# A recommender kernel: categories picked by matmuls, more history tiles fetched row by row, and a loop body of 90 l instead of 45

## The chip, the cores and the metric

One core of a Trainium2 chip runs the kernel. The metric is the device time of one execution in microseconds (us); lower is better. Before the change the median of ten runs was 51,484.07 us (51,445.77 to 51,514.49).

## The reference, cut to what matters

For 16,384 users the kernel computes a small recommender network. `hist` holds 200 (called L, index l) past items for every user.

```python
u, it, c = u_emb[user], i_emb[item], c_emb[cate]          # rows of 64 f32
h = i_emb[hist]                                           # (200, 16384, 64)
feat = concat([h, it, h - it, h * it])
a = dice(feat @ au_W1 + au_b1, au_alpha, axis=1)          # normed over all users
w = a @ au_W2 + au_b2
cur = sum(w * h, axis=0)                                  # over the 200 items
z = concat([u, it, c, cur])
z = dice(z @ W1 + b1, ...); z = dice(z @ W2 + b2, ...)
return z @ W3 + b3
# dice(x): p = sigmoid((x - mean) * rsqrt(var + 1e-8)); x * (p + alpha * (1 - p))
```

The tables of users and items have 100,000 rows of 256 bytes, the table of categories 1,000.

## The kernel before, in words

The users are cut into 128 tiles of 128. A step `k` handles one of 8 columns (`ND`, index c) of 16 tiles (`TD`) for one l: `l, c = divmod(k, ND)`. There are 200 x 8 = 1,600 steps.

**Two ways to fetch rows.** `fetch` (L123 by way of `gather`) asks GpSimd (POOL) for a whole tile with one indirect DMA: 128 rows by a list of indices. `rows_by_address` (L293 and L301) fetches tiles row by row: it loads 16 to 20 addresses into registers (L293, one instruction), and then issues one DMA of 256 bytes per row (L301: a MOVE and the DMA). Half of a step's rows go to SyncE's queue (SP), half to ScalarE's own (ACT). The last tile of the columns in `SIDES = (1, 3, 4, 5, 6, 7)` is fetched in this way, column 5 (`SOMETIMES`) only where l is a multiple of 3 (`EACH`); otherwise its last tile is gathered with indices loaded by `load_side_ids` (L142). So an l has six tiles by address (96 rows a step, 48 per queue) or five (80 rows, 40 per queue). The rows land in three buffers `side` used in turn. `place` waits on ACT until the 128 rows have landed (L311) and copies the tile into the column's buffer (L352). A row for a buffer waits until the tile that lay there has been copied out. There are five column buffers `rows`; POOL fetches for step k + 4 as soon as the transposes have emptied one.

**One step** (`step`), in the order written out by hand (`manual_schedule`), each engine in order:
- POOL gathers the 15 or 16 tiles of step k.
- ACT: `hidden(k-2)` copies px out with the bias (L339), `gate(k-9)` is a sigmoid (L328), `place(k-1)`, then the rows of step k.
- SP: only the rows of step k; at the start of an l the index list of the next (L136), at its third step the addresses (L145).
- DVE (VectorE): four transposes of step k-1's column (`turn`, L156), statistics (L344), `product` (L360), y (L331), the weighted sum (L335, L336).
- PE (TensorE): for k-1 the matmuls into ph and px, for k-9 those into wb (all L161).

At the end of an l `moments` joins the statistics. `scale_and_shift` then has ACT take a square root (L170), for which ACT loads another table of functions and afterwards the old one again, and DVE a reciprocal (L171).

**Stages.** The start gathers all 128 item tiles and turns them. The loop has bodies of `LPB = 45` l, so it runs four times to l = 180; the last 20 l stand after it, and with their last steps the head begins. The head gathers 128 tiles of categories and 128 of users, one column of each in turn, and runs the three layers.

Of the kernel before, what the change touches and what calls it, by code (L numbers as in the profile page):

```python
# [14 lines left out]
P = 128  # L15
# [4 lines left out]
CD = 2 * CH  # L20
LPB = 45
ROWS = 5
# [4 lines left out]
SOMETIMES = 5  # L27
EACH = 3
LOAD = 20
ROW = 4 * D  # L30
U8 = mybir.dt.uint8
# [3 lines left out]
def din_kernel(  # L35
# [75 lines left out]
    idx = [make(f"idx{i}", P, NC, dt=I32) for i in range(IDX)]  # L111
    ids = [make(f"ids{i}", P, NT, dt=I32) for i in range(3)]
    side = [make(f"side{i}", P, D) for i in range(3)]
# [15 lines left out]

    def load_ids(t, v):  # L130
        nc.sync.dma_start(t[:, :NC], columns(v))
        for s in range(NS):
            nc.sync.dma_start(t[:, NC + s : NC + s + 1], col(v[(NC + s) * P : (NC + s + 1) * P]))

    def load_hist_ids(i, l):
# [7 lines left out]

    def load_addresses(i, l):
        nc.sync.dma_start(addr[i], r_hist[ds(l, 1), NC * P :])  # L145

# [20 lines left out]
    def scale_and_shift(mean, var, rstd, shift):  # L167
        n = mean.shape[0]
        std = small.tile([P, 1], F32, tag="std", name="std")
        nc.scalar.activation(std[:n], var, AF.Sqrt, bias=eps[:n])  # L170
        nc.vector.reciprocal(rstd, std[:n])  # L171
        nc.vector.scalar_tensor_tensor(shift, mean, -1.0, rstd, ALU.mult, ALU.mult)

    eps = make("eps", P, 1)
    blk_h = make("blk_h", P, P)
# [13 lines left out]
    def attention_weights():  # L189
        nc.vector.memset(eps, EPS)  # L190
        for t in (blk_h, blk_i, blk_m, blk_p, au_bias, au_al, au_w2):
# [44 lines left out]
    def head_weights():  # L236
# [3 lines left out]
        for e in range(2):  # L240
            for g in range(2):
                r, d = quarter(e, g), ts(e, S)
                nc.sync.dma_start(w1a[r, :, ts(g, ZA)], w1[d, :, :ZA])
                nc.sync.dma_start(w1b[r, :, ts(g, ZB)], w1[d, :, ZA:])
        for g in range(2):
            nc.sync.dma_start(w2a[ts(g, ZA), g * ZA : g * ZA + Z2], W2[:ZA])
            nc.sync.dma_start(b1a[ts(g, ZA)], col(b1)[:ZA])
            nc.sync.dma_start(ala[ts(g, ZA)], col(alpha1)[:ZA])
            nc.sync.dma_start(b1b[ts(g, ZB)], col(b1)[ZA:])
            nc.sync.dma_start(bias2[g * ZA : g * ZA + Z2], col(b2))  # L250
            nc.sync.dma_start(al2[g * ZA : g * ZA + Z2], col(alpha2))
            for j in range(4):
                r = slice(j * S + g * ZB, j * S + (g + 1) * ZB)
                nc.sync.dma_start(w2b[r, j, g * ZA : g * ZA + Z2], W2[ZA:])
                w = j * S + g * ZO
                nc.sync.dma_start(w3[g * ZA : g * ZA + Z2, j, w : w + ZO], W3)
                nc.sync.dma_start(alb[r], col(alpha1)[ZA:])
# [8 lines left out]

    flat = i_emb.rearrange("v d -> (v d)").bitcast(U8)


# [3 lines left out]
    def tiles_by_address(l):  # L273

        round_, i = divmod(l, EACH)
        first = round_ * (EACH * (NS - 1) + 1) + i * (NS - 1) + (i > 0)
        return first, [j for j, c in enumerate(SIDES) if has_side(l * ND + c)]

    def rows_by_address(k):
        l, s = divmod(k, ND)  # L280
        first, tiles = tiles_by_address(l)
        n = len(tiles) * P // ND // 2
        loads = -(-n // LOAD)
        for i, (engine, issue) in enumerate(
            ((mybir.EngineType.SP, nc.sync), (mybir.EngineType.Activation, nc.scalar))
        ):
            r0, end = (2 * s + i) * n, (2 * s + i + 1) * n
            while r0 < end:
                many = min(end - r0, -(-n // loads))
                at0 = tiles[r0 // P] * P + r0 % P  # L290
                while tiles[(r0 + many - 1) // P] * P + (r0 + many - 1) % P != at0 + many - 1:
                    many -= 1
                _, at = nc.values_load_multi_w_load_instructions(  # L293
                    addr[l % 3][:, at0 : at0 + many],
                    engines=(engine,), min_val=0, max_val=ROW * (V - 1),
                    skip_runtime_bounds_check_because="the DMA checks the address against the table",
                )
                for r, a in enumerate(at, r0):
                    m, p = first + r // P, r % P
# [7 lines left out]
                r0 += many  # L307

    def await_rows(m):
        if m in keys:  # L310
            fence = nc.scalar.wait_ge(landed[m % 3], 16 * P)  # L311
            tc.declare_fence(fence.ins, group=keys.pop(m))
            nc.scalar.sem_clear(landed[m % 3])

    def has_side(k):
        l, c = divmod(k, ND)
        return c in SIDES and (c != SOMETIMES or l % EACH == 0)

# [27 lines left out]
    def place(k):  # L346
        if has_side(k):
            l, c = divmod(k, ND)
            first, tiles = tiles_by_address(l)
            m = first + tiles.index(SIDES.index(c))  # L350
            await_rows(m)
            nc.scalar.copy(rows[k % ROWS][:, TD - 1], side[m % 3])  # L352

# [28 lines left out]

    def step(k, last=None):

# [6 lines left out]
        if has(k - 2):  # L391
            hidden(k - 2)
            if ends:
                measure(k - 2)
                moments((k - 2) // ND)
        if has(k - LAG):
            gate(k - LAG)
        if has(k - 1):
            place(k - 1)
        if has(k):  # L400
            rows_by_address(k)
        if has(k - 1):
            turn(k - 1)
        if has(k - 2) and not ends:
            measure(k - 2)
        if has(k - 1):
            product(k - 1)
        if has(k - LAG):
            weights(k - LAG)
            weigh(k - LAG)  # L410

    def steps(l0, n, end):
        for k in range(n * ND):
            l, c = divmod(k, ND)
            if c == 0 and l + 1 < end:
                load_hist_ids((l + 1) % IDX, l0 + l + 1)
                if (l + 1) % EACH:
                    load_side_ids((l + 1) % IDX, l0 + l + 1)
            if c == 2 and l + 1 < end:
                load_addresses((l + 1) % 3, l0 + l + 1)  # L420
            if c == 4 and l + 1 < end:
                scale_addresses((l + 1) % 3)
            step(k)

    with tc.manual_schedule():
        load_ids(ids[0], r_item)
        load_hist_ids(0, 0)
        load_addresses(0, 0)
        load_ids(ids[1], r_cate)
        load_ids(ids[2], r_user)  # L430
        nc.gpsimd.iota(lanes, pattern=[[1, P]], base=P, channel_multiplier=-1)
        attention_weights()
        for t in (*hT, *xs, *side, hm):
            nc.vector.memset(t, 0.0)
        for t in curT:
            nc.vector.memset(t, 0.0)
# [4 lines left out]
        for c in range(1, 2 * ND):  # L441
            nc.vector.tensor_copy(stats[-1 % 3][:, c, :], stats[-1 % 3][:, 0, :])
        scale_addresses(0)
        layer(px, [(blk_m, hm)])

        for c in range(ND + 1):
            if c < ND:
                for n in range(TD):
                    j = column(c, n)
                    gather(rows[c % ROWS], ids[0][:, j : j + 1], n, i_emb)  # L450
            if c:
                transpose(itT[c - 1], rows[(c - 1) % ROWS])
        nc.vector.memset(rows[-1 % ROWS], 0.0)
        head_weights()
# [15 lines left out]

    def head_fetch(k, j):
        c, u = divmod(j, 2)
        for n in range(TD):
            i = column(c, n)
            gather(rows[k % ROWS], ids[1 + u][:, i : i + 1], n, (c_emb, u_emb)[u])

    def head_layer(j):
        c, u = divmod(j, 2)
        if u == 0:
            pairs = ((2, ucT[j % 4]), (1, itT[c]), (3, curT[c]))  # L480
        else:
            pairs = ((0, ucT[j % 4]),)
        layer(px, [(w1a[:, f], t) for f, t in pairs], first=not u, last=u == 1)
        layer(ph[:S], [(w1b[:, f], t) for f, t in pairs], first=not u, last=u == 1)
        if u:
            nc.scalar.activation(za[c], px, AF.Identity, bias=b1a)
            measure_head(0, c, za[c])
            nc.scalar.activation(zb[c // 4][ts(c % 4, S)], ph[:S], AF.Identity, bias=b1b)
            if c % 4 == 3:
                measure_head(1, c // 4, zb[c // 4])  # L490

    with tc.manual_schedule():
        steps(BODY, L - BODY, L - BODY)
        for j in range(2 * ND + 2):
            if j < 2 * ND:
                head_fetch(K + j, j)
            step(K + j, last=K - 1)
            if 1 <= j <= 2 * ND:
                transpose(ucT[(j - 1) % 4], rows[(K + j - 1) % ROWS])
            if j >= 2:  # L500
                head_layer(j - 2)

# [98 lines left out]
```

## Time and profile before

| what | us |
|---|---|
| the profiled execution, in all | 51,433.07 |
| its span, first to last instruction | 51,431.3 |
| median of ten runs | 51,484.07 |
| PE busy | 20,762.5 (40%) |
| DVE busy | 15,101.0 (29%) |
| ACT busy | 4,417.6 (9%) |
| POOL busy | 23,569.5 (46%) |
| first history row on SP | 113.2 |
| last history row on SP | 51,005.4 |

Issuing a DMA does not count as busy. The queue of an engine is written with a q: SPq, ACTq. A row of the table of groups names the line, the engine, the operation, out<-in and its count; after the bar busy time in us and the mean ns of one; after the next bar how long the engine had been idle before it, and what ended that idle time. A row of the waits says who waited for whom, the total in us, how often, and the longest wait. A row of a timeline has start and duration in us, and instructions that follow one another are merged; the bracket at its end is idle time before it.

### The profile page before, as it was taken

The page shows a single profiled execution, that of the slowest core. Times are in us where ns is not written, and L with a number is a line of the kernel's source. Part 1 is how long each engine was busy: PE and PEld are TensorE (multiplying, and loading weights), DVE is VectorE, ACT ScalarE, POOL GpSimd, SP SyncE. Part 2 cuts the span into 40 slices and gives each one's busy share as a digit, 9 for nine tenths or more (in the row PEclk, how much of TensorE's full clock was granted, in tenths as well). Part 3 has the DMA queues.
Part 4 walks back from the last instruction along what each step waited for, and adds up shares of the span by engine and source line. Part 5 has one row for each costly group of instructions (what it writes and reads, how often), then busy time and mean ns, then how long its engine had stood idle before and what let it go on. Part 6 is the DMA issues. An engine that isn't in the chain of part 4 may idle for free. (4 is left out here: it accounts for less than half of the span.)

```text
span 51431.3 us, 423966 instructions
## 1 busy us (share of the span) xinstructions
PE 20762.5 (40%) x38856; PEld 8517.7 (17%) x38856; DVE 15101.0 (29%) x18955; ACT 4417.6 (9%) x4941; POOL 23569.5 (46%) x24922
## 2 busy tenths in 40 slices
PE   3444444443443444334444444344344444434444
PEld 1111111111111111111111111111111111111111
DVE  2222222232222222222222222222222222222223
ACT  0000000000000000000000000000000000000001
POOL 5444444444444444444444444444444444444444
PEclk7666666666766666666666666666666666666667
DMA  0000000000000000000000000000000000000000
GB/s 19 18 17 17 18 17 17 17 17 18 17 18 17 17 18 17 17 17 18 17 17 18 17 17 18 17 17 17 17 17 18 17 17 18 17 17 18 17 17 17
DMA packets 1130924, 894.71 MB, mean 17 GB/s; under 512 B 729024, under 2 KB 729024, under 8 KB 1127896
## 3 DMA queue, kind: packets, MB, share of 16 engines
q0 software_dynamic: 797344, 818.07, 7.2%
q1 hardware_dynamic: 193112, 31.56, 0.3%
q10 hardware_dynamic: 137440, 17.76, 0.2%
q14 instruction: 2722, 22.30, 0.1%
q8 instruction: 306, 5.01, 0.0%
HBM read 865.10 MB, written 0.13 MB: 17 GB/s over the span
## 5 line engine op out<-in xcount | busy, mean ns | idle before, releaser
L123 POOL DMA_INDIRECT rows<-in_L_rec_i_emb,idx x24400 | 23080.0, 946 | 27451.5 <-DVE hT L156 19846.3
L161 PE MATMUL ph<-hT,unit 128*128 128x512 f32 x6404 | 5963.1, 1087 | 30114.0 <-DVE hT L156 29704.1
L335 DVE SCALAR_TENSOR_TENSOR wb<-wb,au_bias,hT 128x1024 f32<-128x1024 f32 x1609 | 2079.8, 1293 | 23201.1 <-remote 20171.3
L161 PEld LDWEIGHTS ph<-hT,unit 128*128 128x128 f32 x6404 | 1798.8, 311 | 33173.9 <-DVE hT L156 32512.6
L156 DVE STREAM_TRANSPOSE hT<-rows 64x512 f32<-64x512 f32 x6404 | 4516.7, 705 | 8958.0 <-ACT rows L352 8814.3
L339 ACT ACTIVATE xs<-px,au_bias 128x1024 f32<-128x1024 f32 x1602 | 1785.1, 1114 | 45384.5 <-issue 40195.8
L161 PE MATMUL px<-hT,blk_h 128*128 128x512 f32 x6404 | 4014.5, 714 | 291.5 <-issue 153.2
L161 PE MATMUL px<-itT,blk_i 128*128 128x512 f32 x6404 | 3417.9, 616 | 0.0
L161 PE MATMUL wb<-xs,blk_x 128*128 128x512 f32 x6436 | 3294.0, 593 | 47.7 <-DVE curT L336 45.5
L161 PE MATMUL wb<-y,blk_p 128*128 128x512 f32 x6436 | 3294.6, 593 | 37.3 <-DVE y L331 30.6
L161 PE MATMUL px<-hm,blk_m 128*128 128x512 f32 x6408 | 3012.9, 592 | 69.9 <-remote 69.9
L344 DVE BATCH_NORM_STATS2 st<-xs 128x6 f32<-128x512 f32 x3204 | 2061.3, 686 | 1959.4 <-ACT xs L339 1586.0
L360 DVE TENSOR_TENSOR hm<-ph,itT 128x1024 f32<-128x1024 f32 x1601 | 1958.0, 1223 | 1727.0 <-PE ph L161 1159.4
L161 PEld LDWEIGHTS px<-hT,blk_h 128*128 128x128 f32 x6404 | 1601.2, 252 | 2779.0 <-issue 2491.6
L336 DVE TENSOR_TENSOR curT<-wb,curT 128x1024 f32<-128x1024 f32 x1609 | 1970.0, 1224 | 54.8
L331 DVE TENSOR_TENSOR y<-pg,xs 128x1024 f32<-128x1024 f32 x1609 | 1953.9, 1214 | 12.6 <-issue 12.5
L328 ACT ACTIVATE pg<-xs,sh,rs 128x1024 f32<-128x1024 f32 x1609 | 1934.1, 1202 | 28.4 <-DVE y L331 13.9
L161 PEld LDWEIGHTS px<-itT,blk_i 128*128 128x128 f32 x6404 | 1388.7, 217 | 1958.0 <-issue 1958.0
L161 PEld LDWEIGHTS wb<-xs,blk_x 128*128 128x128 f32 x6436 | 1224.1, 190 | 1593.1 <-issue 1543.8
L161 PEld LDWEIGHTS wb<-y,blk_p 128*128 128x128 f32 x6436 | 1224.7, 190 | 1583.4 <-issue 1546.4
L161 PEld LDWEIGHTS px<-hm,blk_m 128*128 128x128 f32 x6408 | 1218.1, 190 | 1605.7 <-issue 1534.6
L352 ACT COPY rows<-side 128x64 f32<-128x64 f32 x1068 | 251.2, 235 | 668.3 <-DMA side<-in_L_rec_i_emb 573.9
(155 smaller groups left out, 2148.4 us busy)
## 6 DMA issues: line engine op xcount, KB each, us to landing
side<-in_L_rec_i_emb SPq DMA_DIRECT2D x68288, 0.2 KB
side<-in_L_rec_i_emb ACTq DMA_DIRECT2D x68288, 0.2 KB
rows<-in_L_rec_i_emb,idx POOLq DMA_INDIRECT x24400
idx<-in_r_hist SPq DMA_DIRECT2D x200, 61.0 KB
addrs<-in_r_hist SPq DMA_DIRECT2D x200, 3.0 KB
sidx<-in_r_hist SPq DMA_DIRECT2D x133, 0.5 KB
rows<-in_L_rec_i_emb,sidx POOLq DMA_INDIRECT x133
rows<-in_L_rec_i_emb,ids POOLq DMA_INDIRECT x128
```

The costliest lines, as they stand in the source:

```text
L123: nc.gpsimd.indirect_dma_start(out=dst[:, n, :], out_offset=None, in_=table, in_offset=bass.IndirectOffsetOnAxis(ap=ids, axis=0),)
L156: nc.vector.transpose(by_tile(dst[ts(e, D)], i), of[ts(i, D), :, ts(e, S)])
L161: nc.tensor.matmul(dst[:, ts(i, CH)], lhsT, rhs[:, ts(i, CH)], start=(first and j == 0), stop=(last and j == len(pairs) - 1), skip_group_c ...
L328: nc.scalar.activation(pg, xs[k % XR], AF.Sigmoid, bias=shifts[i], scale=rstds[i])
L331: nc.vector.tensor_mul(y, pg, xs[k % XR])
L335: nc.vector.scalar_tensor_tensor(wb, wb, au_bias2, hT[k % LAG], ALU.add, ALU.mult)
L336: nc.vector.tensor_add(curT[k % ND], wb, curT[k % ND])
L339: nc.scalar.activation(xs[k % XR], px, AF.Identity, bias=au_bias)
L344: nc.vector.bn_stats(stats[l % 3][:, 2 * c + i, :], xs[k % XR][:, ts(i, CH)])
L352: nc.scalar.copy(rows[k % ROWS][:, TD - 1], side[m % 3])
L360: nc.vector.tensor_mul(hm, ph, itT[k % ND])
```

## The change

- `LPB` is 90: the loop runs twice, to l = 180 again.
- `MOST = 2`: column 5's last tile is by address where l % 3 is 0 or 1.
- `place` waits on DVE, and DVE copies the tile. The rows by address are split: SP's come first; the first load of rows on ACT goes ahead of `gate`, the others behind it.
- `scale_and_shift` has DVE compute the reciprocal root: a first guess by a shift of the bits and three Newton steps, no table of ACT.
- The start fetches six tiles of the items by address too (56% of the rows on SP). Categories are not gathered any more: their 1,000 rows lie in SBUF as 8 blocks of 125, DVE compares the categories of 1,024 users with each block's numbers (L496 of the new kernel), and PE multiplies the block with these ones and zeros. The result is kept in DRAM and read back in the head.
- The head gathers users only, five tiles of them by address, and interleaves the columns with the end of the history.

```diff
-LPB = 45
+LPB = 90
+MOST = 2
...
     def scale_and_shift(mean, var, rstd, shift):
-        nc.scalar.activation(std[:n], var, AF.Sqrt, bias=eps[:n])
-        nc.vector.reciprocal(rstd, std[:n])
+        nc.vector.tensor_scalar_add(v, var, EPS)
+        nc.vector.tensor_single_scalar(h.bitcast(I32), v.bitcast(I32), 1, ALU.logical_shift_right)
+        nc.vector.tensor_scalar(
+            rstd.bitcast(I32), h.bitcast(I32), -1.0, float(0x5F375A00), ALU.mult, ALU.add
+        )
+        for _ in range(3):
+            nc.vector.scalar_tensor_tensor(h, rstd, v, rstd, ALU.mult, ALU.mult)
+            nc.vector.tensor_scalar(h, h, -0.5, 1.5, ALU.mult, ALU.add)
+            nc.vector.tensor_mul(rstd, rstd, h)
...
     def await_rows(m):
         if m in keys:
-            fence = nc.scalar.wait_ge(landed[m % 3], 16 * P)
+            fence = nc.vector.wait_ge(landed[m % 3], 16 * P)
...
     def has_side(k):
         l, c = divmod(k, ND)
-        return c in SIDES and (c != SOMETIMES or l % EACH == 0)
+        return c in SIDES and (c != SOMETIMES or l % EACH < MOST)
...
-            nc.scalar.copy(rows[k % ROWS][:, TD - 1], side[m % 3])
+        nc.vector.tensor_copy(rows[k % ROWS][:, TD - 1], side[m % 3])
...
     def step(k, last=None, weighed=()):
...
-        if has(k - LAG):
+        if has(k):
+            ask_hist(k, 0, slice(None))
+            ask_hist(k, 1, slice(0, 1))
+        if k - LAG not in weighed:
             gate(k - LAG)
+        if has(k):
+            ask_hist(k, 1, slice(1, None))
         if has(k - 1):
             place(k - 1)
-        if has(k):
-            rows_by_address(k)
-        if has(k - 1):
             turn(k - 1)
...
+    def pick_categories(q):
+        for b in range(NB):
+            ones = xs[(q * NB + b) % XR][:PB]
+            nc.vector.tensor_scalar(
+                ones, spread[q % SPREAD], values[:PB, b : b + 1], None, ALU.is_equal
+            )
+            for g in range(2):
+                nc.tensor.matmul(
+                    bank[q % 8][ts(g, D)], table[:, b], ones[:, ts(g, CH)],
+                    start=b == 0, stop=b == NB - 1, skip_group_check=True,
+                )
...
         for c in range(ND + 1):
             if c < ND:
-                for n in range(TD):
-                    j = column(c, n)
-                    gather(rows[c % ROWS], ids[0][:, j : j + 1], n, i_emb)
+                fetch_all(c, c, ids[0], i_emb)
+                ask_all(c, 0.56, -NS, NS, addr[2], i_emb)
+                for q in (2 * c, 2 * c + 1):
+                    pick_categories(q)
...
-        steps(BODY, L - BODY, L - BODY)
-        for j in range(2 * ND + 2):
-            if j < 2 * ND:
-                head_fetch(K + j, j)
+        for j in range(ND + 2):
+            if j < ND:
+                fetch_all(K + j, j, ids[1], u_emb)
+                nc.sync.dma_start(category[j % 2], catT[j])
...
+            if j < ND:
+                ask_all(j, SPLIT, first, NS - 1, U, u_emb)
```

## The prediction

> **What bounds the kernel now.** I read the page's table of groups first, then the waits, then the timelines of the queues SP (SyncE) and ACT (ScalarE) in the steady loop. No engine is busy for half the span, so busy time does not name the bound. Two rows of the page:
>
> ```profile
> L123 POOL DMA_INDIRECT rows<-in_L_rec_i_emb,idx x24400 | 23080.0, 946 | 27451.5 <-DVE hT L156 19846.3
> ...
> L352 ACT COPY rows<-side 128x64 f32<-128x64 f32 x1068 | 251.2, 235 | 668.3 <-DMA side<-in_L_rec_i_emb 573.9
> ```
>
> POOL, which gathers whole tiles of 128 rows, stands idle 27,452 us, and 19,846 of them wait for the transposes that free a buffer: it is not the bound. ACT, when it copies a tile fetched row by row, waits 573.9 us for rows to land. The waits of the whole kernel and those of SP's queue alone:
>
> ```profile
> ACT rows L352 <- DMA side<-in_L_rec_i_emb: 573.9, 314, 7.1
> ...
> SPq L301 <- ACT xs L339: 5.9, 23, 0.6
> ...
> SPq L301 <- ACT rows L352: 1.0, 4, 0.3
> ```
>
> ACT waits 314 times for rows that are late; SP waits for nobody (5.9 and 1.0 us in the whole run). So SP issues rows without a stop and is still the late one. Its timeline over three values of l:
>
> ```profile
> 23339.76 0.36 SPq L136 DMA_DIRECT2D idx<-in_r_hist  x1
> 23340.33 0.36 SPq L142 DMA_DIRECT2D sidx<-in_r_hist  x1
> 23342.28 60.25 SPq L301 DMA_DIRECT2D side<-in_L_rec_i_emb  x80
> 23402.74 0.23 SPq L145 DMA_DIRECT2D addrs<-in_r_hist  x1
> 23404.63 179.61 SPq L301 DMA_DIRECT2D side<-in_L_rec_i_emb  x240
> 23584.71 0.36 SPq L136 DMA_DIRECT2D idx<-in_r_hist  x1
> 23586.67 59.25 SPq L301 DMA_DIRECT2D side<-in_L_rec_i_emb  x80
> 23646.21 0.23 SPq L145 DMA_DIRECT2D addrs<-in_r_hist  x1
> 23648.12 179.59 SPq L301 DMA_DIRECT2D side<-in_L_rec_i_emb  x240
> 23828.17 0.36 SPq L136 DMA_DIRECT2D idx<-in_r_hist  x1
> ...
> 24097.37 0.36 SPq L136 DMA_DIRECT2D idx<-in_r_hist  x1
> ```
>
> The idx load opens an l. From one to the next are 244.95 and 243.46 us for an l with five tiles by address (320 rows on SP) and 269.20 us for one with six (384 rows). Rows fill all of it. That is 0.70 to 0.77 us a row, though a row's two instructions last 29 and 225 ns (medians of that line). The rest is lost while POOL gathers: in the first two steps, with POOL gathering almost without a pause, SP needs 180.39 us for 96 rows, 1.9 us each; between bursts of gathers it issues one in 0.32 us. Whatever is added to SP's rows therefore adds time.
>
> **The change, part by part.** All sums are on the profiled execution: span 51,431.3 us, 51,433.07 in all; the median of the ten runs is 51 us above that, so 51 is added at the end.
>
> *More tiles by address.* Column 5 is fetched by address in two l of three instead of one. Of 200 l, those with remainder 1 change: 67. Each gains 64 rows on SP and 64 on ACT and loses one gather (0.945 + 0.30 us between gathers = 1.25 us on POOL, which is idle anyway). The trace shows the very operation, six tiles beside five: 269.20 - 244.2 (mean of the two) = 25.0 us. 67 x 25.0 = **+1,675**. From below, 64 rows at their bare 254 ns are 16.3 us, +1,089; from above, 64 rows at the five-tile l's own 0.75 us (179.61 / 240) are 48 us, +3,210. I take 25.0, since it is measured whole, gathers included.
>
> [...]
>
> *The side ids.* Loading them takes SP from 1.96 us (idx to first row without it) to 2.52: 0.56 us. It happens in 66 l instead of 133: **-38**.
>
> *Bodies of 90.* The loop turns over at l = 45, 90, 135 and ends at 180. There two neighbouring l on SP together take 21, 24, 26 and 41 us more than 269.2 + 245. Afterwards there is one turn (90) and the end: two turns of 24 go, **-48** (bounds -40 and -55).
>
> *Work taken from ACT.* The square root leaves ACT with its table loads: 260.4 + 264.3 us, 59.1 for the roots, 453.1 waiting for var. The copy of a landed tile goes to DVE (251.2), with the wait for it (573.9). Together 1,862 us, 9.3 per l. I cost this at **0**: ACT already leads SP and waits for its rows, so its time comes back as more waiting. In the steps after an l's end, where ACT loses some 4 us to the tables, SP's step is no shorter, and at the start, with POOL gathering throughout, SP issued 11 rows in 30.8 us before ACT issued any (ACT's first row is at 182.97) and 11 in 28.0 us beside ACT. From below: everything counts, -1,862; from above: nothing.
>
> *Work given to DVE.* Per l, twelve small operations for one reciprocal, about 0.16 us each (+1.8), and 5 or 6 copies; their DVE price isn't shown; ACT's 0.235 gives 1,134 x 0.235 = 266 us. DVE is busy 29%, and the transposes behind these copies already wait 8,814 us for ACT's copy. Cost 0; without that cover 266 + 360 = +626. The new wait for landing stands in DVE's order: behind it are the transposes, the statistics, hm, y and the sum into curT; PE, POOL (free buffers) and ACT's hidden two steps later wait for them. In before the same transposes stood behind the same landing by way of ACT, so nothing new is late. SP's rows for a side buffer now wait for DVE's copy instead of ACT's; from the row where a tile is needed to the one that overwrites it lie at least 1.3 steps.
>
> *Gate behind the first load of rows.* Gate moves behind 16 or 20 rows, some 12 us at 0.7 each; y, the products and the sum follow it. DVE idles 23,201 us before that sum, 14.4 per step, and hidden needs none of it. Cost 0, and up to the missing part if that idle time is needed elsewhere.
>
> *Start.* SP's first history row is issued at 113.2 us, its 97th (third step) at 295. Now 8 x 54 item rows come first. At a six-tile step's 33.7 us (269.2 / 8, 48 rows) plus 6 rows each, that is some 290 us, and two history steps are 67: 360; the first 95 us run at the slow pace shown above (the first 76 gathers fill five buffers without a pause), some 70 us more. So some 360 to 430 instead of 295: I take **+100**. The picks of categories (128 comparisons on DVE, 256 matmuls of 0.6 to 1.06 us on PE, at most 271 us) lie beside this. Bounds: 0, and 526 rows at 1.9 us = 1,000, +600.
>
> *Head.* From SP's last history row (51,005) to the end are 426 us. The 256 gathers of users and categories end at 51,284; four column groups then take 14.4 us each on PE, and 87 us follow. Now 8 steps like those of a five-tile l (30.5 us) end at 51,249, 20 us finish the last column, 87 follow, less two pairs of tables: 51,352. **-80** (bounds 0; and -170 if POOL alone paced it with 123 x 1.25 us).
>
> Sum: 1,675 - 38 - 48 + 100 - 80 = +1,609. Span 53,040; with 2 us around it and the 51 to the median: **53,090**.
>
> **Rivals.**
>
> *ACT, not SP, is the pace* (the other side). Then its 1,862 us count whole: 53,090 - 1,862 = 51,230, 0.5% faster. For it: ACT too has no long rest, with 2.3 us of activations besides its rows in each step. Against it: the 314 waits for rows, none the other way. It decides from where ACT's time per l exceeds SP's by more than the 2.9 us it waits now. Chance 0.08, with the like case that the added rows hide in POOL's shadow and only its 67 gathers count.
>
> *The two queues hinder each other.* While gathers run, SP's and ACT's stalls often alternate; if ACT's freed time gives SP half of itself back, 53,090 - 930 = 52,160. For it: both queues slow down together. Against it: the 11 rows in 30.8 us of SP alone. Chance 0.19 (51,590 to 52,750).
>
> *It gets worse than the sum.* The start at 1.9 us a row (+500), or DVE's late copies stopping SP or pushing bursts of gathers together: without DVE's cover +626. 53,450 to 53,700. For it: DVE's order is strict. Against it: the 8,814 us of cover. Chance 0.10.
>
> *The change doesn't do what it says*: gathers by DMA of categories are gone and the counts of rows are fixed at build time, so this can only be by the bodies: if a turn over a longer body costs twice as much, -48 becomes 0, which is within the range.
>
> **How the numbers follow.** Forecast 52,750 to 53,450: 0.60; half given back: 0.19; worse: 0.10; faster by over 0.2% (below 51,381): 0.08; within 0.2%, about what a measurement of this kernel can tell from no change: 0.03. Slower: 0.60 + 0.19 + 0.10 = 0.89. The range 52,000 to 53,500 leaves out the faster side, the smallest part of the half case, and the tail of the worse one: about 0.2.
>
> **What would show it.** Right: idx to idx on SP again 269 and 245 us, now two long to one short; SP still without waits; ACT with longer idle time before hidden. Row pieces under 0.70 us in six-tile l would show that ACT's relief reaches SP. Waits of SP for DVE of over 100 us in total would show the worse case. SP's first history row near 330 us for the start; about 345 us from the last history row to the end for the head. Wrong altogether if the l shorten to below 253 us on average.

## The result and the profile after

The changed kernel takes 53,039.72 us (median of 8 runs, 52,980.07 to 53,049.16) against 51,486.0 before (28 runs): 1.0300 times as long, 95% interval 1.0291 to 1.0309. That is 3% slower, 50 us from the forecast of 53,090. The profiled execution has a span of 53,043.7 us, 1,612 more than before, and takes 53,045.49 in all.

The experiments ran in four groups (1 to 4, 5 to 8, 9 and 10, 11 and 12), each beside runs of the kernel before, which took 51,399 and 51,406 us in the second and third group, but 31,349 and 31,373 us in the first and last; the first three groups name chip 15 and the last chip 12, so one chip gave both times. Numbers are compared within a group only, or between groups with the same time of before; "the 51 ms groups" and "the 31 ms groups" stand for the two below.

The groups of POOL's gathers and of the copy of a landed tile, which is DVE's now (the page after):

```profile
L125 POOL DMA_INDIRECT rows<-in_L_rec_i_emb,idx x24400 | 23079.9, 946 | 29153.7 <-DVE hT L153 21503.4
...
L382 DVE COPY rows<-side 128x64 f32<-128x64 f32 x1146 | 221.9, 194 | 9866.6 <-DMA side<-in_L_rec_i_emb 9860.0
```

POOL's work is the same within 0.1 us and its idle time is 1,702 us longer. The copy costs 0.194 us on DVE (0.235 on ACT before), and the wait for rows is now 9,860 us instead of 573.9: DVE reaches it earlier than ACT did. SP's own longest waits after:

```profile
SPq L684 <- DVE res L675: 125.9, 2, 113.2
SPq L310 <- DVE rows L382: 95.3, 154, 1.2
SPq L249 <- DVE w1b L243: 90.2, 1, 90.2
SPq L318 <- DVE rows L382: 33.0, 140, 0.3
```

L684 stores the result at the very end. L310 and L318 are the history's rows: 128 us in 200 l, so SP still issues almost without a stop. L249 is new: once, for 90.2 us, SP waits before the loop for a memset. SP's timeline over three l after:

```profile
20011.17 0.36 SPq L133 DMA_DIRECT2D idx<-in_r_hist  x1
20012.91 64.74 SPq L318 DMA_DIRECT2D side<-in_L_rec_i_emb  x96
...
20079.39 199.95 SPq L318 DMA_DIRECT2D side<-in_L_rec_i_emb  x288
20279.85 0.36 SPq L133 DMA_DIRECT2D idx<-in_r_hist  x1
...
20548.72 0.36 SPq L133 DMA_DIRECT2D idx<-in_r_hist  x1
20550.69 57.73 SPq L318 DMA_DIRECT2D side<-in_L_rec_i_emb  x80
...
20610.59 185.52 SPq L318 DMA_DIRECT2D side<-in_L_rec_i_emb  x240
20796.63 0.36 SPq L133 DMA_DIRECT2D idx<-in_r_hist  x1
```

From idx to idx: 268.68, 268.87 and 247.91 us, two long and one short. A row costs 0.69 us in the six-tile l (199.95 / 288) and 0.77 in the other, against 0.69 and 0.75 before. A round of three l takes 783.2 us against 759.5 (means of the rounds that hold neither the start nor a turn or the end of a body): some 23.6 us more, which 66.7 rounds make 1,573 of the 1,612 us by which the span grew.

### The profile page after: what moved, and what is told of

It is laid out like the page before. It is cut to its first block, busy times and chain, and to the rows that moved or that the text cites. A ratio compares the mean times of both kernels' runs of the same rounds, so it can differ in the third digit from the quotient of the medians.

```text
span 53043.7 us, 447373 instructions
## 1 busy us (share of the span) xinstructions
PE 21940.3 (41%) x39376; PEld 8798.7 (17%) x39376; DVE 15799.9 (30%) x22435; ACT 3811.0 (7%) x3295; POOL 23376.7 (44%) x24716
## 5 line engine op out<-in xcount | busy, mean ns | idle before, releaser
L158 PE MATMUL wb<-y,blk_p 128*128 128x512 f32 x6440 | 3846.3, 683 | 4577.7 <-DVE y L359 3645.1
L158 PE MATMUL wb<-xs,blk_x 128*128 128x512 f32 x6440 | 3599.1, 643 | 13.3 <-DVE curT L364 13.3
L382 DVE COPY rows<-side 128x64 f32<-128x64 f32 x1146 | 221.9, 194 | 9866.6 <-DMA side<-in_L_rec_i_emb 9860.0
L158 PEld LDWEIGHTS wb<-y,blk_p 128*128 128x128 f32 x6440 | 1349.8, 217 | 6463.5 <-DVE y L359 3884.9
```

The lines of the kernel that those rows point to most:

```text
L158: nc.tensor.matmul(dst[:, ts(i, CH)], lhsT, rhs[:, ts(i, CH)], start=(first and j == 0), stop=(last and j == len(pairs) - 1), skip_group_c ...
```

## The experiments

The theory: SP's issuing of rows, slowed while POOL gathers, sets the pace, and ACT's relief is worth nothing. The rivals: ACT is the pace; or both queues hinder each other.

### 1. The added tiles taken back (31 ms)

```diff
-MOST = 2
+MOST = 1
```

> Only the added tiles are taken back (column 5 by address in one l of three again); bodies of 90, the relief of ACT and the new start and head stay. Theory (SP's rows pace the loop, ACT's relief is worth nothing): the 67 l fall back from about 269 to 245 us, so 53,040 - 1,573 (the rounds of three l in the trace of the changed kernel, 782.8 against 759.2 us) = about 51,470 us, 51,350 to 51,550. Rival (the relief gave half of itself back, and the added tiles cost 930 us more than I charged): 53,040 - 2,500 = about 50,550. Rival (ACT is the pace): 50,100 or less, since the whole relief would show against the kernel before.

Measured: 31,215.1 us, 0.9954 times before (0.9938 to 0.9971). None of the three numbers fits, for all were worked out from 53,040, and the kernel before itself took 31,349 us here. The chain that ended last in this kernel:

```profile
POOL 30%; issue 12%; PE 5%; DMA 3%; DVE 2%; ACTq 2%; ACT 0%; DVEq 0%; POOLq 0%
```

POOL is the pace here: 945 ns a gather and 294 ns between two (7,175.7 us of issue by 24,400), times 122.67 gathers, are 152.0 us, and an l took 153.4 (a third of the median round of 460.2). So all of the change but the added tiles makes the kernel 0.5% faster in this group.

### 2 and 12. Bodies of 45 l, twice (31 ms)

```diff
-LPB = 90
+LPB = 45
```

> Only the bodies are taken back to 45 l; all else stays as changed. Theory: two turns of the loop come back at 20 to 31 us each, 53,040 + 40 to 62 = 53,080 to 53,100 us. Rival (a turn over a body of 90 costs as much more as there are fewer of them): 53,040, no difference.

> The same kernel as in the second experiment: bodies of 45 l instead of 90, all else as changed. Where the kernel before takes about 51,400 us: theory: two turns of the loop come back, at 20 to 31 us each, 52,960 + 40 to 62 = 53,000 to 53,025. Rival (a turn costs nothing beside rows that are late anyway, or twice as much after a body of twice the length): 52,960. Where the kernel before takes about 31,350: 32,147, as before.

Measured: 32,147.43 us (1.0250 times before, 1.0222 to 1.0279), and 32,152.8 in the last group (1.0237, 1.0215 to 1.0258). It repeats, but the kernel with bodies of 90 did not run in a 31 ms group, so the price of a turn by itself isn't measured there. In the trace the twelve l from l = 44 on, where the loop turns for the first time, take 1,898 us, against 1,884 by the steady round of 169.4, 164.0 and 137.6: 14 us a turn. So the changed kernel would take some 32,120 in these groups, 2.4% more than before (an estimate). Beside experiment 1 the added tiles cost some 900 us here. SP's timeline in the same kind of l:

```profile
15123.60 39.07 SPq L318 DMA_DIRECT2D side<-in_L_rec_i_emb  x96
15162.94 0.23 SPq L142 DMA_DIRECT2D addrs<-in_r_hist  x1
15164.56 118.16 SPq L318 DMA_DIRECT2D side<-in_L_rec_i_emb  x288
```

The same rows by the same instructions take 39.07 and 118.16 us instead of 64.74 and 199.95, 0.41 us each, though POOL gathers with hardly a pause (it is busy 23,038.6 of 32,151 us and idle 7,157.1 between one gather and the next).

### 3 and 11. ACT gets its work back, twice (31 ms)

`root_and_shift` is the function of the kernel before, with ACT's square root and DVE's reciprocal; start and head keep the new one. The edit also takes the order of the kernel before back: gate and copy ahead of all of ACT's rows.

```diff
-        scale_and_shift(mean, var, rstds[i], shifts[i])
+        root_and_shift(mean, var, rstds[i], shifts[i])
...
-            place_tile(k, first + tiles.index(SIDES.index(c)))
+            m = first + tiles.index(SIDES.index(c))
+            await_rows(m, nc.scalar)
+            nc.scalar.copy(rows[k % ROWS][:, TD - 1], side[m % 3])
...
-        if has(k):
-            ask_hist(k, 0, slice(None))
-            ask_hist(k, 1, slice(0, 1))
         if k - LAG not in weighed:
             gate(k - LAG)
-        if has(k):
-            ask_hist(k, 1, slice(1, None))
         if has(k - 1):
             place(k - 1)
+        if has(k):
+            ask_hist(k, 0, slice(None))
+            ask_hist(k, 1, slice(None))
+        if has(k - 1):
             turn(k - 1)
```

> ACT gets its work in the loop back: the wait for a landed tile, its copy and the square root, in the order of the kernel before (gate and place ahead of all rows); tiles, bodies, start and head stay as changed. Theory (SP is the pace, ACT waits for rows anyway): 53,040 within 60 us, and ACT waits for landed rows where DVE does now. Rival (ACT is the pace): up to 1,862 us more, 54,900. Rival (the queues hinder each other, half of the time counts): about 53,970.

> The same kernel as in the third experiment: ACT gets the wait for a landed tile, its copy and the square root back, 9.3 us an l. Where the kernel before takes about 51,400 us: theory (SP's rows pace, ACT stays behind it): with 32 rows more of an l ACT paced at 265.8 us on average; less 32 rows at 0.6 us it needs about 247 with an even split, 256 with its work back, and SP 260.9: 52,960 within 100 us. Rival (ACT is as late as SP, so that half of its work counts): 53,900. Rival (all of it counts): 54,800. Where the kernel before takes about 31,350: 33,446, as before.

Measured: 33,445.81 us (1.0665, 1.0630 to 1.0699) and 33,456.43 (1.0652, 1.0625 to 1.0679). Here the rival is right that ACT's time counts, though not all of it. Against the variant with bodies of 45 beside it ACT's work and its old order cost 1,304 us (33,456 - 32,153), although that variant has two turns more. The chain of this kernel in the last group, and then that of the bodies of 45:

```profile
ACTq 36%; issue 9%; POOL 3%; ACT 2%; PE 2%; DVE 2%; DMA 1%; SPq 0%; DVEq 0%; POOLq 0%
```

```profile
ACTq 9%; POOL 9%; issue 6%; PE 3%; ACT 2%; DVE 2%; DMA 1%; SPq 1%; DVEq 0%; POOLq 0%
```

These chains name only 53 and 33% of the span. In that part ACT's queue stands almost alone with its old work; with the relief it shares the end with POOL. A round of three l is 492.2 us with the work and 471.0 without (medians): 21 of the 28 us (3 x 9.3) that I had costed at 0.

### 4. Fewer rows on SP, first form (31 ms)

```diff
-SPLIT = 0.5
+SPLIT = 0.46
```

> SP issues 46 in 100 of the rows instead of half: 44 of 96 and 37 of 80 per step, so 32 fewer per six-tile l and 24 fewer per five-tile l; ACT issues as many more. Theory (SP is the pace): at 0.39 us (25 us for 64 rows) to 0.70 us a row the l shorten by 11 to 20 us on average, 2,300 to 4,100 us in all, 48,900 to 50,700, or less gain if ACT becomes the pace on the way. Rival (ACT is the pace): 2,300 to 4,100 us more. Rival (both queues are held up together by the gathers and it is all rows together that count): 53,040, no difference.

Measured: 43,175.86 us (1.3768, 1.3723 to 1.3813), 11,000 more than experiment 2. No theory asked for that. The lines of its chain:

```profile
ACTq L318 26%; ACTq L310 15%; ACT pg L356 2%; ACT xs L367 2%; DMA side<-in_L_rec_i_emb 0%; DVE hT L153 0%; PE px L158 0%; DVE st L372 0%; PE ph L158 0%; POOL rows L125 0%; PE wb L158 0%; DVE h L176 0%; DVE other L405 0%; DVE mv L401 0%; DVE h L177 0%
```

L310, the load of addresses into registers, has 15% of the span. The split had cut the loads at odd places. With the even split of experiment 12 a load of 16 addresses takes 1.23 us and one of 20 takes 1.45; all of these loads for the history begin on a multiple of four. In the trace of this kernel SP's loads of 18 that begin there take 1.65, and of those that begin elsewhere SP's of 15 take 3.33 and of 19 4.13 (medians of 2,157 and 528). The run tells the price of such loads, and about the split only that ACT sets the pace when it has more to do here.

### 5 and 6. Both kernels again (51 ms)

> The changed kernel itself, beside the kernel before on the chip of this run. On a chip on which the kernel before takes about 31,350 us (as in the first four experiments): theory (POOL paces an l with five tiles by address, ACT one with six): the l of the variant with bodies of 45 (168, 164 and 140 us) and two turns of 20 to 30 us less, so 32,147 - 55 = about 32,090 us, 2.4% slower than before. Rival (a turn of the loop is dearer here, since POOL runs without a pause): 31,900 or less. On a chip on which the kernel before takes 51,486: 53,040.

> The kernel before itself, for its trace on the chip of this run. On a chip with 31,350 us: theory (POOL paces on average, 122.67 gathers at 1.249 us an l): an l of 153.2 us on average, as with the added tiles taken back; SP's MOVEs all at 0.03 us and no instructions in steps of 0.7 us. On a chip with 51,486: as the first trace.

Measured: 52,963.56 us (1.0308, 1.0293 to 1.0322) and 51,375.77 us (a single execution). This group has the times of the first result, with the same l: 267.7, 268.3 and 246.5 us after, 269.7, 245.0 and 244.1 before.

### 7. Five tiles by address in every l (51 ms)

```diff
-MOST = 2
+MOST = 0
...
         load_hist_ids(0, 0)
+        load_side_ids(0, 0)
```

> The changed kernel with five tiles by address in every l (column 5 never). On a chip with 31,350 us before: theory (POOL paces): 123 gathers at 1.249 us instead of 122.67, 31,215 + 83 = about 31,300. Rival (ACT paces, so the fewer rows the better): 30,500 or less. On a chip with 51,486 before, theory (SP's rows pace): 134 l fall by 23.6 us, 53,040 - 3,150 = about 49,900; rival (POOL or DVE paces): 53,000 or more.

Measured: 49,979.2 us, 0.9732 times before (0.9717 to 0.9746). The 134 l fall to 245 us, and the whole by 2,984: 22.3 us a tile, where the rounds had given 23.6. As the theory expected, and it is faster than both kernels: what the change adds is what should go. The same price tells what the rest of the change is worth: without its 67 added tiles at 22.3 us the changed kernel would take 52,964 - 1,492 = 51,472 us, 73 more than before in this group (an estimate). So relief of ACT, work on DVE, gate, bodies, start and head together cost next to nothing here.

### 8. One tile by address (51 ms)

```diff
-SIDES = (1, 3, 4, 5, 6, 7)
-SOMETIMES = 5
+SIDES = (7,)
+SOMETIMES = 7
...
-MOST = 2
+MOST = 3
```

> The changed kernel with only column 7 by address, one tile per l, 8 rows on SP and 8 on ACT per step, 127 gathers on POOL. On a chip with 31,350 us before: theory (POOL paces): 4.33 x 1.249 x 200 = 1,080 us more than with the added tiles taken back, about 32,300. On a chip with 51,486 before: theory (rows on SP pace there, and POOL idles): POOL becomes the pace, 32,300 to 33,500, 18,000 us faster than before. Rival (while POOL gathers every engine is held up, whatever the rows): 40,000 or more.

Measured: 42,195.04 us, 0.8213 times before (0.8200 to 0.8225), the fastest in these groups of the kernels that leave nothing out, but 9,000 us from what POOL's pace would give. Its l take 207.5 us, and POOL needs 127 x 1.24 = 157. The chain no longer names SP:

```profile
another core or an unknown queue 24%; PE 12%; DVE 12%; issue 5%; POOL 1%; DMA 0%; DVEq 0%; ACT 0%; POOLq 0%; ACTq 0%
```

With few rows left something other than issuing them takes over, and a quarter of the chain goes to releasers that the profile cannot name. The time is what the rival asked for (40,000 or more), and the waits and timelines of ACT and POOL fit it:

```profile
ACT xs L367 <- remote: 22998.0, 797, 59.0
```

```profile
15261.07 0.94 POOL L125 DMA_INDIRECT rows<-in_L_rec_i_emb,idx  x1 [0.30 <-issue]
15279.19 0.94 POOL L125 DMA_INDIRECT rows<-in_L_rec_i_emb,idx  x1 [17.17 <-DVE hT L153]
```

```profile
15266.46 1.11 ACT L367 ACTIVATE xs<-px,au_bias 128x1024 f32<-128x1024 f32 x1 [27.54 <-remote]
```

The gather at 15261.07 is the last of a burst of 32. ACT stands idle 27.54 us before it copies px out, though PE's matmuls of that time end by the profile at 15250.4, and goes on 4.4 us after the burst. It is nearly always so: of the 797 times that ACT stands over 20 us before this copy (23,026 us in all), 792 end within 6 us after a burst of gathers; in the 31 ms groups' experiments 1 and 12 it never stands that long. So in this group the bursts seem to hold up ACT as well as the rows, as the rival says; no run tests that alone, and how they would do it stays open.

### 9. Fewer rows on SP, loads on multiples of four (51 ms)

```diff
-SPLIT = 0.5
+SPLIT = 0.46
...
-        many = round(n * split)
+        many = 4 * round(n * split / 4)
...
-            at = [r0 + (end - r0) * i // loads for i in range(loads + 1)]
+            at = [r0 + (end - r0) // 4 * i // loads * 4 for i in range(loads)] + [end]
```

> SP issues 44 of 96 and 36 of 80 rows of a step, ACT 52 and 44: 32 rows of each l go from SP to ACT, in loads of addresses that all begin on a multiple of four (loads that began elsewhere took 3.2 to 4.2 us instead of 1.23 to 1.45 in the first variant of this experiment). Where the kernel before takes about 51,400 us: theory (SP is the pace): 32 rows at 0.39 to 0.70 us are 12.5 to 22 us an l, 48,500 to 50,500. Rival (ACT is the pace): 2,500 to 4,400 us more. Rival (both queues are held up together, and all rows together count): 52,960, no difference. Where the kernel before takes about 31,350: ACT paces the l with six tiles, 32 rows at 0.34 us for 133 l, 1,450 us more than the changed kernel, about 33,500.

Measured: 53,944.6 us, 1.0493 times before (1.0475 to 1.0510), about 980 us slower than the changed kernel. The theory asked for a gain of 2,460 at least and missed; the rivals asked for no difference and for a loss of 2,500 or more, and missed too. The chain of the changed kernel in the group before, and then of this one:

```profile
SPq 31%; issue 19%; ACTq 1%; PE 1%; DMA 1%; DVE 1%; another core or an unknown queue 0%; ACT 0%; DVEq 0%
```

```profile
ACTq 31%; issue 17%; ACT 3%; DVE 2%; PE 1%; DMA 0%; another core or an unknown queue 0%; POOL 0%; DVEq 0%; SPq 0%; POOLq 0%
```

Eight to ten rows in a hundred of SP's are enough to hand the end from SP's queue to ACT's. The l take 300.1, 272.9 and 224.9 us: the six-tile ones grow by 32 and 5, the five-tile one shrinks by 22. The five-tile l shrinks with the same rows in all, so it isn't all rows together that count. SP is the pace of the changed kernel, but with ACT close behind: in an l with six tiles an even split is near the balance. An uneven one in the five-tile l alone was not tried.

### 10. Half of the gathers (51 ms)

This kernel leaves out every second gather of the history. Eight are left in every step, also where the kernel has 15 (0, 2, ..., 14), so an l has 64 instead of 122 or 123.

```diff
-        for n in range(TD - has_side(k)):
+        for n in range(0, TD - has_side(k), 2):
```

> Every second gather of the history is left out (eight or seven per step instead of 16 or 15); rows by address and all arithmetic stay. Where the kernel before takes about 51,400 us: theory (SP's rows pace, and they are slow because POOL gathers): a six-tile l at the bare pace is 384 x 0.34 + 24 x 1.25 = 160 us against 268 now; half the gathers give half of the difference, some 50 us an l, about 43,000. Rival (a row is slow by itself, or for want of DMA): 52,960, no difference. Where the kernel before takes about 31,350: theory (ACT paces the six-tile l): within 1,000 us of the changed kernel's 32,090; rival (POOL paces): far below, 27,000.

Measured: 39,111.72 us, in a single execution. SP's timeline:

```profile
15166.67 0.36 SPq L133 DMA_DIRECT2D idx<-in_r_hist  x1
15168.64 40.68 SPq L318 DMA_DIRECT2D side<-in_L_rec_i_emb  x80
...
15340.17 0.36 SPq L133 DMA_DIRECT2D idx<-in_r_hist  x1
...
15540.79 0.36 SPq L133 DMA_DIRECT2D idx<-in_r_hist  x1
```

A five-tile l takes 173.50 us and a six-tile one 200.62, with the same rows: 0.52 to 0.54 us each instead of 0.69 to 0.77. So in this group the rows are slow because of the gathers. The traces say the same by place: in the changed kernel of experiment 5, SP's rows follow each other every 1.16 us inside a burst of gathers and every 0.46 outside (means). It is not gathering alone: in experiment 12 nearly all rows fall inside bursts and follow each other every 0.43. Whether POOL's issuing or the transfers that it starts slow the rows is not shown. The gain is larger than half of the gap (68 us in an l with six tiles, not 50). SP still waits little (128.3 us at L310, 25.7 at L318) and issues rows all the time.

## Why the prediction was right, point by point

- **What bounds the kernel.** SP's queue, slowed by gathers: right in the 51 ms groups (chain SPq 31%; experiments 7 and 10); the DMA engines were busy 0.08 of the loop before (23,342 to 24,097 us of its trace). It was too simple in two respects. ACT stands right behind SP (experiment 9): I read ACT's 314 waits for rows as a lead of ACT's and named its size, 2.9 us an l, only in a rival. And POOL's bursts seem to hold up ACT too, which shows once the rows are few (experiment 8).
- **More tiles and side ids**, 1,675 - 38 = 1,637: 1,573 by the rounds (which hold all that changed in the loop), 1,492 by half of experiment 7. Right mechanism, 4 to 10% too much. The 25.0 us were one comparison of neighbouring l; experiment 7 gives 22.3 over many.
- **Bodies of 90**, -48: the traces give -65. After, two neighbouring l together take 20 us more than 269.2 + 245 at the turn at 90 and 28 at the end, against 21, 24, 26 and 41 before. No run in a 51 ms group tests it alone.
- **Work taken from ACT**, 0: nothing in the 51 ms result speaks against it, since all but the added tiles comes to some 73 us (experiment 7), but no run there tests it alone. In the 31 ms groups it fails: taking the work back costs some 1,300 us (experiments 3 and 11). Had my result fallen into such a group, the rival "ACT is the pace" would have been nearer the truth (experiment 12 has ACT's queue and POOL at 9% of the span each); the kernel would still have been slower, as the added tiles put their rows on ACT too.
- **Work given to DVE**, 0: right as far as the sum shows. SP's waits for DVE's copy are 128 us in pieces of at most 1.2, and the copy is 222 us in all. By the letter the 128 us are the sign that I had set for the worse case (over 100 us in total); the time shows no worse case, so that sign was set too low.
- **Gate behind the first load**, 0: not tested alone. Nothing of the size of a step shows up in the rounds.
- **Start**, +100: here it was 214, the largest error of the sum. The 97th history row leaves SP at 509.5 us instead of 295, the first at 442.2 instead of near 330. Most of the missing part is a wait that I did not list: the loads of the head's weights stand on SP ahead of the loop and wait 90.2 us for DVE's memset of w1b (L243), which now comes behind the memsets that follow the picks of categories. In experiment 10 this wait is 52.7 us and the first history row leaves 37.7 us earlier, at 404.5. (The bound of +600 was also a slip: 1,000 - 295 is 705.) Another part may be the loads of 18 and 14 addresses, half of which begin off a multiple of four. In experiment 9, where none does and SP has 52 rows a step instead of 54, the index load of the second l comes 31 us earlier (406.95 against 437.53 in experiment 5); 10 of them are a shorter wait at L249 (85.9 against 96.1).
- **Head**, -80: -91. From SP's last history row (52,708.8) to the end are 335 us instead of 426.
- **The rivals.** Half of the relief given back would have been 52,160, and ACT as the pace 51,230: the time excludes both for the 51 ms groups, and experiment 7 the like case of added rows that cost nothing. The worse case had the start as one of its reasons, and that came in part (+114), but DVE's late copies did not stop SP.
- **The signs.** Two long l and one short, 268.7, 268.9 and 247.9 us, came as I had said. ACT idles less before hidden (30,881 us instead of 45,385), not longer; its idle time moved ahead of gate (17,658 instead of 28). Rows under 0.70 us in a six-tile l would have shown that ACT's relief reaches SP: they took 0.69, but 199.69 / 288 = 0.69 before too, so it shows nothing.
- **The sum.** 1,573 - 65 + 214 - 91 = 1,631 against the measured 1,612. That the forecast's 1,609 is so close is partly luck: the start was too low by 114, the tiles too high by 64, the bodies by 17 and the head by 11. The 50 us between forecast and result are the 51 added for the median: after, the profiled execution lies 6 us above it. And both kernels were measured in the condition of the first trace; in the other one POOL and ACT would have set the pace.

**What stays open.** Why the same program issues rows at 0.41 us in one group and at 0.7 in another. The traces show how, not why: while POOL gathers, SP's MOVEs take up to 1.48 us in a 51 ms group, and 9,346 of 73,767 take over 0.5 (experiment 5), all but 7 of them inside a burst of gathers or within 6 us after it; with half the gathers it is 4,096 (experiment 10); in a 31 ms group none takes over 0.06. The traces also hold fewer records of DMAs landing in the 51 ms groups, 264,109 for the changed kernel (experiment 5) against 694,670 for the bodies of 45 (experiment 12). The times without a profile are within 0.2% of those with one, in both.

## What to carry to other kernels

Where an engine's issuing is the pace, the trace may hold the very operation beside its neighbour without it (here l with six and with five tiles): the difference between whole stretches priced the edit better (25.0 us against the 22.3 of experiment 7) than sums of instructions did (16 to 48 us). Before costing the relief of a second engine at nothing, find out how far it is behind the first; a shift of 8 to 10 rows in a hundred between the two showed it here (experiment 9). And have the kernel before run beside every experiment: here the bound itself differed from group to group, and only that run showed it.

## What the runs showed of the hardware that was not expected

- One program on one core took 31.3 or 51.4 ms, the same within a group to 0.8%. The gathers last 944 ns in both (means, experiments 5 and 12); SP's MOVEs beside them take at most 0.06 us in one and up to 1.48 us in the other.
- A load of 16 to 20 addresses into registers took 1.23 to 1.65 us where it began on a multiple of four (medians, experiments 12 and 4), and one of 15 or 19 took 3.33 or 4.13 where it began elsewhere (medians, experiment 4, whose kernel took 43,176 us instead of some 32,150).
- With 58 of 122 gathers left out, an l with six tiles took 68 us less, 63% of its gap to 160 us (experiment 10). The 160 are that experiment's estimate, 384 rows at 0.34 us and 24 loads at 1.25; experiment 12's timeline gives 0.33 a row with the loads at 1.23.
- With few rows, ACT stood idle through POOL's bursts of gathers in a 51 ms group: of its 797 stands of over 20 us ahead of the copy of px, 792 end within 6 us after a burst (experiment 8).
